# Block places of a group: one load of 14 from memory, five loads of three into ScalarE's registers, in place of two loads of seven each

## The chip, the cores and the metric

The kernel runs on one core of a Trainium2 chip. The metric is the time of one execution on the device in microseconds; the time before is the median of eight runs, 3712.68 us (3709.05 to 3725.59).

## The reference, cut to what matters

12,500 nodes with 32 features each, 400,000 edges sorted by their target `dst`. Two graph layers follow one another, each with a residual and a normalisation over the features:

```python
# layer 0: spline convolution, nine weight matrices blended per edge
messages = einsum('ek,ei,kio->eo', basis(edge_attr), x[src], weight)
out = zeros.at[dst].add(messages) / max(degree, 1)
x = layernorm(x + out + x @ root_w.T + root_b)
# layer 1: relational convolution, four bases weighted by the edge's type
for b in range(4):
    out = out + segment_sum((x[src] @ W[b]) * edge_type_weight[b][edge_type], dst)
x = layernorm(x + out)
```

The hard part is `x[src]`: every edge reads the row of its source node.

## The kernel before, in words

Most edges are cut into groups of 2304 (128 partitions by 18 columns, `GE`), 125 groups in all (`NG`). The setup sorts each group's edges by source; then the edges of a block of seven times 128 nodes lie next to each other. Layer 0 takes 92 of the groups (the first 33 are left to another path, the near work below), layer 1 all 125.

`layer(which)` loops over the groups. For each group `take(g)` makes 14 blocks (`NBL`), and for each block `block(k)` does this:

- At the first block of each half (`LOADS`, seven blocks each), SyncE's queue (SP) starts a load of the half's slot rows, `sl` (L1308, 1064 KB, two buffers), and a load of its seven block places, `hd` (L1312, 28 bytes, two buffers). Then ScalarE's queue loads the seven places from `hd` into its registers (L1314), with the order hint to stand behind the last move but one.
- At the first block of each quarter (`PIECES`, three or four blocks) VectorE compares the slot rows with the partition's number, which gives the 0/1 matrix `s` (L1324).
- TensorE multiplies seven node tiles by `s` into one of three PSUM banks (L1334): the rows of the block's sources, in sorted order.
- ScalarE moves the bank into `yt` (L1341), at a place that is known only when the kernel runs. A register holds it: two register operations split it into the place in `yt` and the place in the bank, and the move uses both. This is "the move" below, 14 a group.

`use(g)` takes the finished `yt` in three pieces of six columns, spread over the blocks of the next group: TensorE turns the piece back to edges (`y`, L1354), VectorE compares edges with targets (`hot`, L1366) and multiplies by the edges' coefficients (`outer`, L580), and TensorE sums by target (`agg`, L1389). After the third piece ScalarE copies the sum out (`agg_sb`, L599), TensorE applies the weights (L605), ScalarE and VectorE store the result in three parts (`rows`, L587 to L590), and later "hit" matmuls (L742) add it to the nodes' totals. The near work gathers the edges that belong to no group by indirect DMA (L124) and sums them by matmuls of L1079; it runs beside both layers.

The instructions of each engine are put in order by a planner when the kernel is built, from the order of the calls, the buffers and the hints (`issue_after`). Each engine then runs its list in order: an instruction that waits holds up all behind it. A load into registers occupies ScalarE's own queue. Where the load is behind a waiting copy, it starts when that copy has started.

The names that matter: `heads` (pool of `hd`), `begins` (the registers by block), `moves` (the list of moves), `banks` (three), `LOADS`, `PIECES`, `begin_d` (the places in memory, 125 rows of 14).

## Time and profile before

| | |
|---|---|
| median of 8 runs | 3712.68 us |
| the profiled execution | 3717.11 us |
| its span, first to last instruction | 3714.6 us |
| TensorE / VectorE / GpSimd / ScalarE busy | 77% / 81% / 70% / 57% |
| layer 0, 776 to 2270 us: TensorE / ScalarE busy | 1411 / 877 us of 1494 |
| layer 1, 2320 to 3680 us: TensorE / ScalarE busy | 1241 / 724 us of 1360 |
| loads of places into registers (L1314) | 434, median 967 ns |
| loads of places from memory (L1312) | 434 |
| moves (L1341) | 3038, median 383 ns |

The busy time of an engine counts what its datapath does. Loads into registers and register arithmetic run in the engine's queue (ACTq for ScalarE); they show in the chain and in the answers on a single line, not in the busy time. Where the profile says that an engine was idle until "issue", its queue was occupied with such things.

### The profile page before, as it was taken

How to read it: one execution, taken by the hardware profiler on the slowest of the kernel's cores; microseconds unless marked ns; L12 is line 12 of the kernel's file. 1: busy time of each engine (PE TensorE's matmuls, PEld its weight loads, DVE VectorE, ACT ScalarE, POOL GpSimd, SP SyncE). 2: the span in 40 equal slices, each digit the busy share in tenths (PEclk: the TensorE clock that was granted, in tenths of full speed). 3: DMA queues.
4: the chain of work that ended last, by engine and by line, in shares of the span. 5: the costliest groups of instructions: out<-in, count | busy, mean ns of one | idle time of the engine just before them, and what ended most of it. 6: DMA issues, size and time to landing. Idle time of an engine off the chain costs nothing.

```text
span 3714.6 us, 110703 instructions
## 1 busy us (share of the span) xinstructions
PE 2868.4 (77%) x40674; PEld 2458.3 (66%) x40674; DVE 3000.6 (81%) x5847; ACT 2103.4 (57%) x5610; POOL 2598.3 (70%) x2393
## 2 busy tenths in 40 slices
PE   2222221159999999999999997889999999989997
PEld 1121111147777777777777775888888888888886
DVE  5899979579899999986777775777777778878786
ACT  4688866345556665655566553555555555555553
POOL 4767777727777777777777771676777777777730
PEclk9955555579999999999999997999999999999998
DMA  4000001155556555555555453666776677777663
GB/s 93 14 11 14 14 14 14 31 176 160 166 166 180 167 167 172 176 164 152 155 168 154 146 165 108 212 214 207 218 224 214 213 229 219 220 218 219 204 224 100
DMA packets 202776, 564.88 MB, mean 152 GB/s; under 512 B 75796, under 2 KB 141944, under 8 KB 146170
## 3 DMA queue, kind: packets, MB, share of 16 engines
q1 hardware_dynamic: 123924, 511.77, 43.6%
q0 software_dynamic: 75888, 40.38, 6.3%
q8 instruction: 319, 5.23, 0.6%
q10 hardware_dynamic: 2410, 5.59, 0.6%
q14 instruction: 235, 1.93, 0.2%
HBM read 531.76 MB, written 25.76 MB: 150 GB/s over the span
## 4 chain that ended last, share of the span: by engine, by line
PE 53%; POOL 7%; ACT 5%; issue 5%; DVE 4%; ACTq 3%; DMA 3%; SPq 0%; POOLq 0%; DVEq 0%
PE agg L1389 26%; PE bank L1334 19%; POOL n_xg L124 7%; ACT yt L1341 3%; ACTq L1314 3%; PE y L1354 2%; PE n_bank L1079 1%; DMA n_xg<-in_x_dram,n_idx 1%; PE wg L876 1%; ACTq L1341 1%; ACT agg_sb L599 1%; PE wg L1105 1%; PE n_sum L742 1%; DMA z_dram<-n_z 1%; DVE hot L1376 1%
## 5 line engine op out<-in xcount | busy, mean ns | idle before, releaser
L124 POOL DMA_INDIRECT n_xg<-in_x_dram,n_idx x1469 | 1628.5, 1109 | 561.5 <-issue 433.1
L1341 ACT ACTIVATE yt<-bank x3038 | 1162.7, 383 | 553.7 <-PE bank L1334 320.9
L1389 PE MATMUL agg<-hot,outer 128*128 128x82 f32 (+1 forms) x7812 | 1413.4, 323 | 5.1 <-DVE hot L1376 3.8
L1334 PE MATMUL bank<-s,x 128*128 128x108 bf16 (+3 forms) x21266 | 1174.6, 202 | 189.4 <-ACT yt L1341 159.6
L1334 PEld LDWEIGHTS <-x 128*128 128x128 bf16 x21266 | 1007.4, 98 | 339.1 <-issue 226.1
L124 POOL DMA_INDIRECT n_xg<-z_dram,near_i x875 | 938.6, 1073 | 383.9 <-issue 256.9
L1389 PEld LDWEIGHTS agg<-hot,outer 128*128 128x128 f32 (+1 forms) x7812 | 1071.8, 181 | 128.9 <-DVE hot L1376 6.1
L1324 DVE TENSOR_SCALAR s<-sl,row 128x1824 bf16<-128x1824 int16 x868 | 679.1, 784 | 147.9 <-PE bank L1334 119.0
L1376 DVE TENSOR_TENSOR hot<-agg,hot_b 128x984 f32<-128x984 f32 x276 | 324.9, 1177 | 105.2 <-ACT agg_sb L599 56.4
L580 DVE TENSOR_TENSOR outer<-co,y 128x768 f32<-128x768 f32 x375 | 354.5, 945 | 0.0
L1079 PE MATMUL n_bank<-n_w,n_xg 128*32 128x72 f32 x3024 | 140.8, 256 | 199.0 <-DMA n_xg<-in_x_dram,n_idx 96.0
L1366 DVE TENSOR_TENSOR hot<-in_order,y 128x492 f32<-128x492 bf16 x375 | 248.0, 661 | 50.4 <-PE y L1354 46.6
L599 ACT ACTIVATE agg_sb<-agg 128x82 f32<-128x82 f32 (+1 forms) x217 | 64.5, 297 | 332.3 <-PE agg L1389 316.5
L1079 PEld LDWEIGHTS n_bank<-n_w,n_xg 128*32 128x32 f32 x3024 | 81.3, 121 | 244.6 <-DMA n_xg<-in_x_dram,n_idx 115.2
L1374 ACT ACTIVATE hot<-hot_b 128x492 f32<-128x492 bf16 x276 | 167.3, 606 | 116.7 <-PE agg L1389 91.3
L1354 PE MATMUL y<-add,yt 96*128 96x32 bf16 x3906 | 218.9, 177 | 4.1 <-DVE outer L580 4.1
L245 ACT ACTIVATE in_order<-src,thr 125x2304 bf16<-125x2304 int16 x97 | 213.9, 2205 | 0.7
L1354 PEld LDWEIGHTS <-yt 96*128 96x128 bf16 x3906 | 179.8, 98 | 13.5 <-issue 7.4
L580 DVE TENSOR_TENSOR outer<-co_b,y 128x384 f32<-128x384 f32 x276 | 151.0, 547 | 30.1 <-ACT outer L1373 28.2
L1062 DVE TENSOR_TENSOR n_w<-n_basis,n_hot 128x864 f32<-128x864 f32 x162 | 136.8, 850 | 18.7 <-PE n_bank L1079 18.4
L1259 DVE SCALAR_TENSOR_TENSOR co<-eq,etw_sb,co 128x180 f32<-128x180 f32 (+1 forms) x364 | 128.0, 390 | 2.0
L739 DVE TENSOR_SCALAR n_hit<-cols,place_of 82x128 bf16<-82x128 f32 (+2 forms) x301 | 100.3, 346 | 19.4 <-PE n_sum L742 19.1
(266 smaller groups left out, 2826.7 us busy)
## 6 DMA issues: line engine op xcount, KB each, us to landing
sl<-slots SPq DMA_DIRECT2D x434, 1064.0 KB
n_xg<-in_x_dram,n_idx POOLq DMA_INDIRECT x1469
n_xg<-z_dram,near_i POOLq DMA_INDIRECT x875
z_dram<-n_z SPq DMA_DIRECT2D x49, 256.0 KB
hd<-begin_d SPq DMA_DIRECT2D x434, 0.0 KB
co_d<-co SPq DMA_DIRECT2D x13, 360.0 KB
co<-co_d SPq DMA_DIRECT2D x13, 360.0 KB
args_t<-args_d SPq DMA_DIRECT2D x25, 90.0 KB
```

The lines of the kernel that those rows point to most:

```text
L124: return nc.gpsimd.indirect_dma_start(out=xg, out_offset=None, in_=table, in_offset=bass.IndirectOffsetOnAxis(ap=idx, axis=0))
L245: nc.scalar.activation(t, of[:NG], AF.Sign, bias=bias, scale=scale, accum_out=total)
L580: return nc.vector.tensor_tensor(t[:, :c, at:at + k * D].rearrange("p c (k d) -> p c k d", k=k), co[:, :, :, None].to_broadcast([P, c, k, D]),
L1079: nc.tensor.matmul(o, self.xg[i][:, at[0], at[1], :], v, start=True, stop=True, tile_position=(0, j * D))
L1324: nc.vector.tensor_scalar(s[:, :n], slots_of[k][:, :n], row, None, op0=ALU.is_equal)
L1334: nc.tensor.matmul(bank[:, AHEAD + a:AHEAD + b], parts[:, w * M3:w * M3 + P], s[:, off_[j]:off_[j + 1]], start=(j == 0), stop=(j == B - 1) ...
L1341: moves.append(nc.scalar.activation(yt[:M3, ds(to, LONG)], bank[:M3, ds(place, LONG)], AF.Copy))
L1354: nc.tensor.matmul(y[:, c, :], yt[:M3, k * P:(k + 1) * P], add3[:M3, :], start=True, stop=True)
L1366: nc.vector.tensor_tensor(hot.rearrange("p c (m i) -> p c m i", i=2), rel.to_broadcast([P, SUB, MAXR // 2, 2]), (col_ps if which else col_ ...
L1374: nc.scalar.activation(spread[:, :, 0, :], hot, AF.Copy)
L1376: nc.vector.tensor_tensor(spread[:, :, 1:, :], b0[:, :, :, None].to_broadcast([P, SUB, 2, MAXR]), hot[:, :, None, :].to_broadcast([P, SUB, ...
L1389: near.behind = nc.tensor.matmul(agg[0], t[:, c, :], v, start=(k == 0), stop=(k == CH - 1)).ins
```

## The change

The places get a load of their own: at the first block of a group, `hd` takes all 14 from memory in one DMA. Into ScalarE's registers they go three at a time, at blocks 0, 3, 6, 9 and 12 (the last time two). The slot rows stay in two loads a group. The order hint of the register load is the same as before. Nothing that is computed changes.

```diff
-            co_of = {}
+            co_of, hd_of = {}, {}
...
                 def block(k):
+                    if k == 0:
+                        hd_of[g] = heads.tile([1, NBL], I32, name="hd")
+                        nc.sync.dma_start(hd_of[g], begin_d[g:g + 1, :])
+                    if k % 3 == 0:
+                        n = min(3, NBL - k)
+                        with tc.issue_after(moves[-2].ins) if len(moves) > 1 else ExitStack():
+                            _, v = nc.values_load_multi_w_load_instructions(
+                                hd_of[g][:, k:k + n], engines=[mybir.EngineType.Activation],
+                                min_val=0, max_val=GE * BANK + AHEAD,
+                                skip_runtime_bounds_check_because="counted, and bounded")
+                        begins.update(zip(range(k, k + n), v))
                     for k0, k1 in LOADS[which]:
                         if k == k0:
...
-                            hd = heads.tile([1, NBL // 2], I32, name="hd")
-                            nc.sync.dma_start(hd[:, :k1 - k0], begin_d[g:g + 1, k0:k1])
-                            with tc.issue_after(moves[-2].ins) if len(moves) > 1 else ExitStack():
-                                _, v = nc.values_load_multi_w_load_instructions(
-                                    hd[:, :k1 - k0], engines=[mybir.EngineType.Activation],
-                                    min_val=0, max_val=GE * BANK + AHEAD,
-                                    skip_runtime_bounds_check_because="counted, and bounded")
-                            begins.update(zip(range(k0, k1), v))
                             slots_of.update({i: sl[:, (i - k0) * WS:] for i in range(k0, k1)})
```

In the built order ScalarE's list has 1085 register loads of places where it had 434, and SP's list 217 loads of `hd` where it had 434. The planner also places other work anew: in layer 1 the copy of `agg` stands ahead of the eighth move in 106 of 125 groups before, and ahead of the second move in 98 of 125 groups after.

## Prediction

> **What bounds the kernel now.** I read the page's busy table first, then the chain that ended last, then the two layers apart. TensorE carries the largest share of the chain, 53%. The setup before about 776 us holds no step of this change, so only the two layers count: 92 groups of 14 blocks from about 776 to 2270 us (layer 0) and 125 from about 2320 to 3680 us (layer 1).

> ```profile
> PE 2868.4 (77%) x40674; PEld 2458.3 (66%) x40674; DVE 3000.6 (81%) x5847; ACT 2103.4 (57%) x5610; POOL 2598.3 (70%) x2393
> ...
> PE 53%; POOL 7%; ACT 5%; issue 5%; DVE 4%; ACTq 3%; DMA 3%; SPq 0%; POOLq 0%; DVEq 0%
> ```

> The chain of waits, taken for 2330 to 3640 us alone, has this sum by line. The register load of the block places (ACTq L1314) is 6.0% of 1310 us there, 79 us, and the moves behind it another 4.9%. The longest waits of TensorE in the same stretch, and in 790 to 2260 us, name one cause each time: a block can't start because ScalarE hasn't emptied its bank.

> ```profile
> by line: PE bank L1334 38.2%; PE agg L1389 38.0%; ACTq L1314 6.0%; ACT yt L1341 4.9%; PE y L1354 3.6%; issue 2.9%; ACT agg_sb L599 2.0%; PE n_bank L1079 1.4%; ACTq L1341 1.4%; PE n_sum L742 0.4%; DVE hot L1366 0.2%; DVE outer L580 0.2%; DVE
> ```

> ```profile
> PE bank L1334 <- ACT yt L1341: 111.9, 126, 1.4
> ```

> ```profile
> PE bank L1334 <- ACT yt L1341: 44.4, 98, 1.9
> ```

> So layer 1 has one such wait a group (126 in 120 groups or so), 0.89 us each; layer 0 has half as much a group. The timeline of one group of layer 1 shows how it comes about.

> ```profile
> 3002.81 0.24 ACT L599 ACTIVATE agg_sb<-agg 128x82 f32<-128x82 f32 x1 [1.72 <-PE agg L1389]
> ...
> 3004.10 0.80 ACT L1341 ACTIVATE yt<-bank  x2 [1.05 <-issue]
> ...
> 3004.54 0.44 PE L1334 MATMUL bank<-s,x 128*128 128x108 bf16 x7 [1.10 <-ACT yt L1341]
> ```

> ScalarE stands at the copy of agg until TensorE is done, then its queue loads seven places (968 ns, unseen by the busy time), and only then the eighth move of the group runs. TensorE has three banks, so its eleventh block waits for that move, 1.10 us here. In the built order of before, 106 of 125 groups of layer 1 have exactly this sequence: copy of agg, load, eighth move. The group's other load lies behind the last move of the group before, while TensorE does agg products, and no wait follows it.

> **What one load costs.** Two pairs of moves of ScalarE with a load between them:

> ```profile
> L1314 ACTq TENSOR_LOAD <-hd x1: 962/962/962, 3006.6 to 3006.6; - x1
> ```

> ```profile
> 3006.19 0.80 ACT L1341 ACTIVATE yt<-bank  x2
> 3007.88 0.80 ACT L1341 ACTIVATE yt<-bank  x2 [0.90 <-PE bank L1334]
> ```

> The gap is 0.90 us; between moves without a load it is 0.03 (five moves take 2.04 us, 0.414 apart, 0.383 each). (The view names a block as releaser; the block had come, and the load ended at 3007.57.) So a load of 7 values costs ScalarE 0.87 us, 0.09 less than its 0.96, since the queue starts it while the move ahead still runs.

> The trace has no load of three. It is bounded by the loads it has: all 434 of hd take about 967 ns for seven values, and the one-value loads at the end of the kernel are these.

> ```profile
> L1314 ACTq TENSOR_LOAD <-hd x434: 956/967/1969, 776.0 to 3674.8; - x145
> ```

> ```profile
> L1626 SPq TENSOR_LOAD <-again x1: 553/553/553, 2331.3 to 2331.3; - x1
> ...
> L1626 ACTq TENSOR_LOAD <-again x1: 288/288/288, 3704.8 to 3704.8; - x1
> L1626 DVEq TENSOR_LOAD <-again x1: 543/543/543, 3705.4 to 3705.4; - x1
> ```

> Lower end 288 ns (count doesn't matter, the short row is the price), upper end 967 ns (count doesn't matter, the long row is). In between: a straight line through ScalarE's own two rows gives (967-288)/6 = 113 ns a value, so 514 ns for three and 401 for two; a line from the other queues' 553 gives 69 ns a value and 691 for three. I take 514, since both its rows are ScalarE's; it costs 0.42 us in the row of moves, the load of two 0.31.

> [...]

> **The change part by part.**
> 1. Loads on ScalarE a group: before 2 x 0.87 = 1.74 us, after 4 x 0.42 + 0.31 = 1.99 us, so +0.25. Bounds: 5 x 0.20 = 1.0 (-0.74) and 5 x 0.87 = 4.35 (+2.61). The register arithmetic of the moves is unchanged (three instructions for each of 3038 moves); 651 loads are added (434 become 1085).
> 2. Layer 1, what goes: in the built order of after, the copy of agg comes ahead of the second move in 98 of 125 groups, and no load stands directly behind it. The wait of the eleventh block goes, -0.89 us a group. From the eighth block on TensorE now does three blocks, then y and agg (12 agg matmuls at about 0.11 us each, 1.34, and y 0.16): 3 x 0.28 + 1.50 = 2.3 us, against three moves and a load on ScalarE, 3 x 0.414 + 0.42 = 1.66. ScalarE catches up there.
> 3. Layer 1, what comes: blocks 1 to 8 have no such pause between them. The seventh block needs the fourth move, and ScalarE has ahead of that, from the copy of agg on: the copy 0.27, two moves 0.83, rows 0.21, a load 0.42, the fourth move 0.38 and 0.05 to TensorE, 2.16 us. TensorE meanwhile has four blocks 1.12, y 0.16, the weights 0.14, and on average 0.15 of hit matmuls: 1.57, of which 0.25 passed before the copy began. That leaves 0.6 to 0.85 us, and up to 1.15 where rows waits for the weights' matmul; the near work (1736 matmuls of L1079 in 125 groups, in runs of 28) takes some away where it falls in between. I take 0.69, so -0.20 us a group, times 125: -25 us. The bounds are 0.4 (-61 us) and 1.15 (+32).
> 4. Layer 0: TensorE is busy 1397 of 1470 us, and ScalarE has more idle time. The 44.4 us of waits stand against 184 loads x 0.87 = 160 us, so 28% of load time reaches TensorE. +0.25 x 92 x 0.28 = +6 us.
> 5. The DMAs of places: 434 of 7 become 217 of 14, each some 0.24 us of SP's issue. In the trace SP sits behind the register loads (575.6 us in 217 waits in layer 1) and nobody waits for that but the slot rows. Now the places wait for the last of five loads, ahead of the second slot load of the group in SP's built order; that load's data are used more than half a group later. VectorE waited for slot rows only 14.6 us in 23 waits in layer 1, so the cover is thin there but it holds: 0. Bounds: -15 us, and 0.7 us a group later, +88, if every part of it showed.

> Sum: -25 + 6 = -19 us. The profiled execution took 3717.1 us (span 3714.6), 4.4 above the median of the runs shown; its sum would be 3698, and against the median of 3712.7 it is 3694.

> **Rivals.**
> - Forecast, 3694, chance 0.53. Its own range is 3665 to 3712, most of the bounds in part 3 with loads near 0.5 us.
> - The price of three values lies midway between the two lines, at 0.60 us: each load costs 0.51, a group 2.49 (+0.75). The seventh block's wait grows by 0.09, so layer 1 gives -14, layer 0 +0.75 x 92 x 0.28 = +19: 3718, no change that shows within its own spread. Chance 0.12.
> - Slower: a load costs ScalarE nearly the same whatever it carries, and the load ahead of the fourth move becomes the wait that the eleventh block had. It decides from about 0.57 us for three values. At 0.69: a group pays 4 x 0.60 + 0.53 = 2.93 (+1.19), layer 0 +31, layer 1 -25 + 0.18 x 125 = -3, together 3741. At 0.967 ScalarE itself bounds layer 1: 14 moves 5.8, loads 4.35, copy and rows 0.7, near work 0.3, 11.2 us and some waiting that it can't fill, against 10.9 now (1360 us over 125); I put +0.85 us a group, 106, and layer 0 +2.61 x 92 x 0.28 = 67: 3886. For it speak the other queues' 490 to 553 ns for one value; against it ScalarE's 288. Chance 0.31, a third of it near the top.
> - The wait of SP: slot rows late in layer 1, +0.3 us a group, 3731. Chance 0.04.
> - That the change doesn't do what it says is excluded by the built order: 1085 loads, 217 DMAs.

> **How the numbers follow.** A measurement of this kernel can tell about 0.2%, 7.4 us, from no change. Below 3705 lies the forecast but for the upper end of its own range, and a little of the second case where the bounds of part 3 and of part 5 help it: faster, 0.53. Same, the rest of these two: 0.13. Slower, the third and fourth, less what of them stays near 3712: 0.34. The range goes from 3660 to 3770; it leaves out the top of the slower case (0.10) and as much beyond the gain of the forecast and in the tails.

> **What would show it.** Right: ScalarE's register loads near 514 ns for three; the wait of TensorE's blocks for moves in layer 1 below 112 us, now at the seventh block and not the eleventh; layer 0 within 10 us. Wrong: loads of 600 ns and more; more waits of blocks for moves in layer 0; VectorE waiting for slot rows for over 30 us.

## The result and the profile after

The changed kernel takes 3758.39 us, the median of 14 runs (3741.21 to 3783.26); beside it the kernel before takes 3714.45 (40 runs). The ratio is 1.0121, interval [1.0108, 1.0134]: slower, where the forecast was faster. Eight of the runs below (e5 to e8 and e13 to e16) were made on two other chips, where the kernel before itself took 6206 and 6162 us and TensorE, VectorE and ScalarE stand still together again and again in every profile, for 5 to 43 us (near 4110 us of e6 TensorE stood 15.1 us, ScalarE 19.4, VectorE 23.6; the cause is not known); of these runs the ratios to that kernel are given, and otherwise only their groups at full clock are read.

The profiled execution took 3767.13 us (span 3764.6), 50.0 more in span than before. From the start of a layer's first move to that of its last, layer 0 went from 1478.1 to 1502.6 us (+24.5), layer 1 from 1404.5 to 1439.5 (+35.0); the setup and what lies between and behind the layers took 9.5 less. The busy table and the chain of the page:

```profile
PE 2870.0 (76%) x40674; PEld 2484.7 (66%) x40674; DVE 3008.8 (80%) x5847; ACT 2153.0 (57%) x5610; POOL 2564.4 (68%) x2393
...
PE 58%; ACT 9%; ACTq 5%; issue 4%; DVE 3%; DMA 2%; SPq 0%; POOL 0%; DVEq 0%
```

The work is the same; ScalarE and its queue have a larger part of the chain. The chain for 2330 to 3640 us by line, then TensorE's longest waits in 2340 to 3640 us and in 790 to 2260 us (sum, times, longest):

```profile
by line: PE agg L1391 36.5%; PE bank L1336 31.9%; ACT yt L1343 7.9%; ACTq L1308 4.7%; issue 4.0%; PE y L1356 3.7%; ACTq L1343 1.7%; ACT agg_sb L599 1.6%; PE n_bank L1079 1.5%; ACT rows L587 1.3%; DMA sl<-slots 1.3%; PE wg L605 1.2%; PE n_su
```

```profile
PE bank L1336 <- ACT yt L1343: 127.2, 168, 1.5
```

```profile
PE bank L1336 <- ACT yt L1343: 95.9, 200, 2.7
```

Blocks still wait for moves and for hardly anything else. In layer 0 these waits doubled (44.4 us before), in layer 1 they grew a little (110.9 before, in the same stretch). And this is what one register load costs (minimum, median, maximum, ns):

```profile
L1308 ACTq TENSOR_LOAD <-hd x1085: 493/703/1990, 769.5 to 3730.4; - x181
```

That is the median of all loads: three values take 706 ns, two 497. The prediction had 514 and 401. All loads of places together occupy ScalarE's queue for 733 us, before 432.

**Layer 0.** The timeline of ScalarE at a change of groups, the load there, and TensorE's fourth block:

```profile
848.14 0.61 ACT L1376 ACTIVATE hot<-hot_b 128x492 f32<-128x492 bf16 x1 [1.95 <-PE agg L1391]
849.16 0.38 ACT L1343 ACTIVATE yt<-bank  x1 [0.41 <-PE bank L1336]
```

```profile
L1308 ACTq TENSOR_LOAD <-hd x1: 709/709/709, 848.1 to 848.1; - x1
```

```profile
849.60 0.44 PE L1336 MATMUL bank<-s,x 128*128 128x108 bf16 x7 [0.66 <-ACT yt L1343]
```

The copy waits 1.95 us for TensorE's sums, the load behind it in the queue starts with the copy and ends at 848.85, and only then comes the group's first move, for which the fourth block waits 0.66 us. In the built order of before, the load stands ahead of that copy here: at the same change of groups it started at 848.4, 3.0 us ahead of the group's first block, and the fourth block waited 0.14:

```profile
L1314 ACTq TENSOR_LOAD <-hd x1: 967/967/967, 848.4 to 848.4; - x1
```

```profile
851.58 0.62 ACT L1374 ACTIVATE hot<-hot_b 128x492 f32<-128x492 bf16 x1 [1.11 <-PE agg L1389]
...
852.10 0.36 ACT L1341 ACTIVATE yt<-bank  x1
```

```profile
851.38 1.58 PE L1334 MATMUL bank<-s,x 128*128 128x108 bf16 x28
```

There the first move follows the copy at once, and the four blocks run as one row. Fourth blocks waited some 21 us in layer 0 before and 60 after; tenth blocks 2.4 and 23.

**Layer 1.** One group, ScalarE's timeline, the load in it, and the seventh block of TensorE:

```profile
3022.48 0.24 ACT L599 ACTIVATE agg_sb<-agg 128x82 f32<-128x82 f32 x1
3022.74 0.80 ACT L1343 ACTIVATE yt<-bank  x2
3023.95 0.19 ACT L587 ACTIVATE rows<-wg 82x32 bf16<-82x32 f32 x1 [0.41 <-PE wg L605]
3024.98 1.22 ACT L1343 ACTIVATE yt<-bank  x3 [0.83 <-ACT rows L587]
```

```profile
L1308 ACTq TENSOR_LOAD <-hd x1: 707/707/707, 3024.0 to 3024.0; - x1
```

```profile
3025.42 0.85 PE L1336 MATMUL bank<-s,x 128*128 128x108 bf16 x14 [1.09 <-ACT yt L1343]
```

The wait is where the prediction put it, at the seventh block, and for its reason: the copy of agg, two moves, rows waiting for the weights' product, and behind it the load (0.83 us without a move). It came to some 118 us in all, where the eleventh block's had been 109.

That alone is no loss: the groups of layer 1 at full clock take 10.82 us (105 of them), before 10.83 (114). The 35 us are in the others. From the fifth group on, those touched by a lowered TensorE clock are 15 with 13.56 us, before 6 with 12.37: 15 x 2.74 = 41 us more than at full clock, before 6 x 1.54 = 9. The half-clock time in layer 1, counted from 40 us behind its first move, is 123 us, before 35. (In the kernels before and after the clock is lowered in the layer's first group too, from 2288 to 2329 and from 2305 to 2343 us.) The view by stretches (busy us and instructions of the five engines, then the granted clock):

```profile
2359.70:2366.50 6.80, 6.80 (x67) 6.80 (x63) 4.47 (x7) 2.20 (x7) 5.28 (x6) 0.50 0.45 146
2366.50:2373.30 6.80, 5.40 (x93) 5.07 (x92) 3.66 (x7) 3.58 (x12) 5.28 (x6) 1.00 0.68 199
2373.30:2380.20 6.90, 6.90 (x70) 6.90 (x66) 4.39 (x7) 2.29 (x8) 5.38 (x6) 0.51 0.52 150
2380.20:2387.00 6.80, 5.39 (x93) 5.06 (x91) 3.73 (x7) 3.62 (x12) 5.28 (x6) 1.00 0.69 196
```

The clock drops to 0.50 for 6.8 us and is back at 1.00 for 6.8, again and again. At half clock TensorE is busy all the time, at full clock it idles 1.4 us of 6.8. Behind the layer's first group all the lowered stretches in the trace of the kernel after are 3.41, 6.83, 10.24 or 23.89 us long, that is 1, 2, 3 or 7 times 3.41.

### The profile page after: what moved, and what is told of

The parts are those of the page before. It is cut to its first block, busy times and chain, and to the rows that moved or that the text cites. A ratio compares the mean times of both kernels' runs of the same rounds, so it can differ in the third digit from the quotient of the medians.

```text
span 3764.6 us, 110775 instructions
## 1 busy us (share of the span) xinstructions
PE 2870.0 (76%) x40674; PEld 2484.7 (66%) x40674; DVE 3008.8 (80%) x5847; ACT 2153.0 (57%) x5610; POOL 2564.4 (68%) x2393
## 4 chain that ended last, share of the span: by engine, by line
PE 58%; ACT 9%; ACTq 5%; issue 4%; DVE 3%; DMA 2%; SPq 0%; POOL 0%; DVEq 0%
PE agg L1391 31%; PE bank L1336 18%; ACT yt L1343 6%; ACTq L1308 3%; PE y L1356 2%; PE n_bank L1079 2%; ACTq L1343 2%; ACT hot L1376 1%; PE wg L876 1%; PE wg L605 1%; PE wg L1105 1%; PE n_sum L742 1%; DMA sl<-slots 1%; ACT agg_sb L599 1%; ACT rows L587 0%
## 5 line engine op out<-in xcount | busy, mean ns | idle before, releaser
L1391 PE MATMUL agg<-hot,outer 128*128 128x82 f32 (+1 forms) x7812 | 1447.3, 327 | 5.4 <-DVE hot L1378 3.7
L1336 PE MATMUL bank<-s,x 128*128 128x108 bf16 (+3 forms) x21266 | 1188.5, 203 | 265.0 <-ACT yt L1343 237.1
L1336 PEld LDWEIGHTS <-x 128*128 128x128 bf16 x21266 | 1026.1, 100 | 397.9 <-issue 321.9
L124 POOL DMA_INDIRECT n_xg<-z_dram,near_i x875 | 919.0, 1050 | 457.5 <-issue 255.7
L1391 PEld LDWEIGHTS agg<-hot,outer 128*128 128x128 f32 (+1 forms) x7812 | 1110.3, 185 | 132.9 <-issue 7.0
L580 DVE TENSOR_TENSOR outer<-co,y 128x768 f32<-128x768 f32 x375 | 354.5, 945 | 0.0
L1079 PE MATMUL n_bank<-n_w,n_xg 128*32 128x72 f32 x3024 | 131.0, 255 | 181.5 <-DMA n_xg<-in_x_dram,n_idx 78.1
L1079 PEld LDWEIGHTS n_bank<-n_w,n_xg 128*32 128x32 f32 x3024 | 77.8, 121 | 221.4 <-DMA n_xg<-in_x_dram,n_idx 92.6
L1356 PEld LDWEIGHTS <-yt 96*128 96x128 bf16 x3906 | 174.8, 98 | 10.9 <-issue 5.2
L580 DVE TENSOR_TENSOR outer<-co_b,y 128x384 f32<-128x384 f32 x276 | 151.1, 547 | 36.4 <-ACT outer L1375 35.1
L1062 DVE TENSOR_TENSOR n_w<-n_basis,n_hot 128x864 f32<-128x864 f32 x162 | 136.4, 848 | 18.5 <-PE n_bank L1079 13.8
L599 ACT ACTIVATE agg_sb<-agg 128x82 f32<-128x82 f32 (+1 forms) x217 | 64.6, 297 | 123.4 <-PE agg L1391 117.0
L742 PEld LDWEIGHTS <-n_hit 82*128 82x128 bf16 (+1 forms) x905 | 72.7, 108 | 64.8 <-DVE n_hit L739 51.9
```

The source lines that it names most:

```text
L124: return nc.gpsimd.indirect_dma_start(out=xg, out_offset=None, in_=table, in_offset=bass.IndirectOffsetOnAxis(ap=idx, axis=0))
L580: return nc.vector.tensor_tensor(t[:, :c, at:at + k * D].rearrange("p c (k d) -> p c k d", k=k), co[:, :, :, None].to_broadcast([P, c, k, D]),
L1079: nc.tensor.matmul(o, self.xg[i][:, at[0], at[1], :], v, start=True, stop=True, tile_position=(0, j * D))
L1336: nc.tensor.matmul(bank[:, AHEAD + a:AHEAD + b], parts[:, w * M3:w * M3 + P], s[:, off_[j]:off_[j + 1]], start=(j == 0), stop=(j == B - 1) ...
L1356: nc.tensor.matmul(y[:, c, :], yt[:M3, k * P:(k + 1) * P], add3[:M3, :], start=True, stop=True)
L1391: near.behind = nc.tensor.matmul(agg[0], t[:, c, :], v, start=(k == 0), stop=(k == CH - 1)).ins
```

## The experiments

"Half clock" below is the time in layer 1 at the lowered clock, counted as above, and every layer time is of a run's profiled execution.

**e1_sizes: what a load costs by its size and start.** The places are loaded by a plan that changes with the group:

```diff
-                    if k % 3 == 0:
-                        n = min(3, NBL - k)
+                    plan = ((14,), (7, 7), (3, 3, 3, 3, 2), (4, 4, 4, 2), (5, 5, 4), (6, 8), (1, 13), (9, 5))[g % 8]
+                    at = [sum(plan[:i]) for i in range(len(plan))]
+                    if k in at:
+                        n = plan[at.index(k)]
```

> One DMA of 14 places a group, as in the changed kernel, but the register loads carry other numbers of values in turn, by group: 14 / 7,7 / 3,3,3,3,2 / 4,4,4,2 / 5,5,4 / 6,8 / 1,13 / 9,5. It measures the price of one load by its number of values. Known: 285 ns for one, 497 for two, 703 for three, 967 for seven. Theory A (a price that rises by some 209 ns a value while few are asked for, and more slowly beyond): four between 0.75 and 0.92 us, five to eight near 0.97 to 1.1, fourteen between 1.2 and 1.9. Rival B (a straight line through one and seven, the prediction's): 4 at 0.63, 5 at 0.74, 14 at 1.76. Rival C (a line of 209 ns a value from one on, and seven an oddity): 4 at 0.91, 5 at 1.12, 6 at 1.33, 8 at 1.75, 14 at 3.0.

One execution, 3773.17 us. Medians of the register loads, by number of values and first value, us:

| values, start | us | values, start | us |
|---|---|---|---|
| 1 at 0 | 0.288 | 7 at 0 | 0.971 |
| 2 at 12 | 0.500 | 7 at 7 | 1.550 |
| 3 at 0, 3, 6, 9 | 0.702 to 0.710 | 8 at 6 | 1.750 |
| 4 at 0, 4, 8 | 0.310 to 0.328 | 9 at 0 | 0.788 |
| 4 at 10 | 0.920 | 13 at 1 | 2.824 |
| 5 at 0 / 5 / 9 | 0.552 / 1.132 / 1.117 | 14 at 0 | 1.241 |
| 6 at 0 | 0.771 | | |

**e2_merge7 and e3_two_dmas: the two parts of the change apart.** e2 is the change with one DMA of 14 places, but two register loads of seven (n = 7 at blocks 0 and 7). e3 has the loads of three, but two DMAs of seven places.

```diff
-                    if k % 3 == 0:
-                        n = min(3, NBL - k)
+                    if k % 7 == 0:
+                        n = 7
```

> The DMA part of the change alone: one DMA of 14 places a group, and still two register loads of seven. The built order is nearly that of the kernel before. If the register loads carry the whole loss: within 0.2% of the kernel before, 3714 us, with the wait of TensorE's blocks for moves at about 111 us in layer 1 and 44 in layer 0. If the later load of places or the slot rows behind it in SP's queue carry part of it: over 3722.

> The register part alone: the places come in two DMAs of seven a group, both started at the group's first block, and go to the registers three at a time. The built order is nearly that of the changed kernel. If the register loads carry the whole loss: 3758 us, 1.012 of before, within its own spread of 3741 to 3783. If the merged DMA carries part: below 3740.

e3: ratio 1.0210 [1.0159, 1.0261], layer 0 1500.5, layer 1 1447.7 us, half clock 132, waits as in the kernel after (58.2 us at fourth blocks of layer 0, 122.2 at seventh blocks of layer 1). So the register loads make the loss without the merged DMA. (That e3 is 0.9% slower still than the kernel after, 3766 to 3808 us in four executions, stays unexplained.) e2: 4023.81 us, ratio 1.0846 [1.0820, 1.0872], the slowest of all. It was no clean test of the DMA, for its second load starts at value 7 and takes 1.55 us; layer 1 took 1692.7 us, 598 of them at half clock.

**e6, e10 (merge7_at8): the DMA alone. e7 (seven_at1): the price alone.** In merge7_at8 a group has 16 places of storage, one DMA, and two loads of seven at values 0 and 8. In seven_at1 the kernel before has its second seven stored from value 1 of their tile; its order of instructions is that of before.

```diff
-                            hd = heads.tile([1, NBL // 2], I32, name="hd")
+                            o = 1 if k0 else 0
+                            hd = heads.tile([1, 8], I32, name="hd")[:, o:]
```

> The kernel before with only the DMA part of the change: one DMA of 16 places, two register loads of seven at offsets 0 and 8, both multiples of four, each expected at 0.965 us as before. Theory P (the DMA part is worth nothing; in the run with the merged DMA and the second load at offset 7 the loss came from that load's 1.55 us): 3700 to 3725, register-load total within 10 us of 432, waits at the eleventh block in layer 1 as before (105 to 115 us). Rival R (the merged DMA itself, its landing or its place on SP's queue, costs time): over 3750, and the waits would name the DMA queue.

> The DMA part alone, again on another chip: one DMA of 16 places a group, two register loads of seven at offsets 0 and 8. Theory P: the DMA part is worth nothing, 3700 to 3725, register-load total within 10 us of 432, wait at the eleventh block in layer 1 of 105 to 115 us. Rival R (the merged DMA costs time by itself): over 3750, the waits naming the DMA.

> The kernel before with both DMAs and its order unchanged, but the second seven places of a group stored from value 1 of their tile, so that their register load reads seven values from a start that is no multiple of four: by the run with mixed sizes 1.55 us instead of 0.965. Theory P (price of the load alone, 0.58 us a group in the stall at the eleventh block, and then the granted clock): 3980 to 4040, layer 1's half-clock time 500 to 650 us, wait at the eleventh block 1.3 to 1.5 us a group. Rival R (the merged DMA was the cause in the earlier run): 3700 to 3730. A third case, that the stall lengthens but the clock doesn't follow: 115 groups of layer 1 times 0.58 = 67 us, 3775 to 3790.

e10: 3726.17 us, ratio 1.0034 [1.0023, 1.0044]; e6 1.0006 [0.9987, 1.0024]. Layer 1 is as before (1406.7 us, eleventh block 108.1, half clock 46), but not so layer 0: 1493.5 us, with 59.2 us at fourth blocks. With the places' DMA called at the group's first block, ahead of the slot rows, the planner puts the group's first load behind the waiting copy (in e3, with two DMAs called there, it does too), and that costs a third of a per cent. Rival R falls, and theory P is missed by a little: the DMA part is not quite worth nothing.

e7, on one of those two chips: 1.0380 [1.0353, 1.0406]; 111 of 120 groups of layer 1 are touched by the lowered clock (61 in e6, on that chip). The time by which e7 was expected at 3980 to 4040 can't be read there; that the price alone costs, with one order and no merged DMA, can. The cleanest pair is e2 and e10, with the same order of instructions on TensorE and ScalarE. Here are the loads of both in layer 0 and 1 together, then the stretch 2340 to 3580 us, first e2, then e10:

```profile
L1308 ACTq TENSOR_LOAD <-hd x434: 956/1532/2271, 775.1 to 3982.3; - x145
```

```profile
L1310 ACTq TENSOR_LOAD <-hd x434: 957/966/1722, 772.7 to 3690.1; - x145
```

```profile
2340.00:3580.00 1240.00, 1092.73 (x15785) 1051.00 (x15785) 791.69 (x1422) 538.18 (x1639) 740.80 (x707) 0.82 0.58 177
```

```profile
2340.00:3580.00 1240.00, 1130.46 (x19450) 1068.79 (x19449) 968.04 (x1756) 659.42 (x2008) 928.68 (x866) 0.99 0.71 217
```

Every second load takes 0.58 us longer (e2's 1532 is the middle of two kinds, 0.97 and 1.55). Over 125 groups of layer 1 that is 73 us; layer 1 grew by 286, and the clock fell from 0.99 to 0.82. The longer wait accounts for 73 us once, and the clock came with some three times as much.

**e8, e11 (filler): is it the pause that lowers the clock?** e2 with eight more products in the place where TensorE waits; nothing uses their result.

```diff
+            if layer:
+                at[0] = wide()[:MAXR, :D]
+                for _ in range(8):
+                    filled[layer] = nc.tensor.matmul(at[0], s[:k, :MAXR], w1_sb, start=True, stop=True)
...
+                        with tc.issue_after(filled[1].ins) if k == 10 and 1 in filled else ExitStack():
```

> The kernel with the merged DMA and two loads of seven at offsets 0 and 7 (4024 us, layer 1 1693 us, 598 us of it at half clock), with eight extra matrix products in each of layer 1's groups that read the aggregate and whose result nothing uses, placed in the order just ahead of the eleventh block, where TensorE waits for the second load. Theory S (the idle stretch of about 1.4 us in each group is what brings the lowered clock, and the lowered clock is what costs the time): half-clock time in layer 1 under 300 us and time under 3880. Rival T (the clock is lowered for another reason, or the products merely add to the time): half-clock time over 450 us and time of 4000 or more.

> Again on another chip: the kernel with the merged DMA and two loads of seven at offsets 0 and 7 (4024 us, 598 us of layer 1 at half clock), with eight extra matrix products a group of layer 1, whose result nothing uses, where TensorE waits ahead of the eleventh block. Theory S (the idle stretch of some 1.4 us a group brings the lowered clock): half-clock time in layer 1 under 300 us, time under 3880. Rival T (the clock is lowered for another reason, or the products only add): half-clock time over 450 us, time 4000 or more.

e11: 3868.48 us, ratio 1.0411 [1.0377, 1.0445], half clock 121 us: more work for TensorE, and 155 us less than e2. Theory S holds: with the pause filled, most of the half clock goes (598 us in e2), and with e2 against e10 (598 and 46) that makes the pause what lowers the clock in these runs. (The planner also moved the weights' product from behind the tenth block to behind the fourteenth, so the order is not e2's throughout. e8: 1.0250 [1.0222, 1.0279].) A rule of how much pause is too much did not come out: TensorE's idle time in layer 1's groups and the half clock stood at 112 and 35 us in the kernel before, 139 and 123 after, 142 and 33 in e9 below, 77 and 121 in e11. The length of the single pause fits better: from the fifth group of layer 1 on, the traces have 5 pauses of TensorE over 1.2 us before, 39 after, 1 in e9, none in e17 and 92 in e2. But the 1.2 us are picked afterwards, and e11 has 4, so this is a hint and no rule.

**e5, e9 (padded): five cheap loads.** The places are stored three to a stretch of four, and each load takes four values from a multiple of four.

```diff
-                                hd_of[g][:, k:k + n], engines=[mybir.EngineType.Activation],
+                                hd_of[g][:, k // 3 * 4:k // 3 * 4 + 4], engines=[mybir.EngineType.Activation],
```

> The kernel after, with the 14 places of a group stored three to a stretch of four values (20 places of storage, one DMA), so that each register load reads four values from a start that is a multiple of four: five loads in the same places of the order, each expected at 0.325 us by the run with mixed sizes, instead of 0.703 for three and 0.497 for two. Theory P (the time of one register load sets the loss, first by layer 0's moves, then by a longer stall in layer 1 that lowers the granted clock): register loads fall from 733 to about 340 us; layer 0's waits of the block products for moves are at most 44 us, layer 1's under 70; the half-clock time of layer 1 falls from 123 to under 40 us; time 3640 to 3690. Rival Q (the number of loads or their places between the moves sets the loss, whatever one costs): 3740 to 3780, waits as in the kernel after.

> The kernel after with the 14 places of a group stored three to a stretch of four values, so that each of the five register loads reads four values from a start that is a multiple of four; a repeat on another chip, because on the first one the kernel before itself took 6206 us and all four engines but GpSimd stood without instructions for stretches of some 20 us. There the loads took 0.314 us each. Theory P (the time of one register load sets the loss): layer 0's waits of the block products for moves at most 44 us, layer 1's under 70, half-clock time of layer 1 under 40 us, time 3640 to 3690. Rival Q (the number of loads or their places set it): 3740 to 3780, waits as in the kernel after.

> The kernel with five loads of four values (3756 us, loads of 0.314 us), its order of instructions unchanged on TensorE and ScalarE, but with the places stored from value 1, so that no load starts at a multiple of four: by the run with mixed sizes each then takes 0.92 us. Theory P (in layer 0 the group's first load stands on TensorE's path, so the wait of the fourth block is the load's time less some 0.05 us): that wait rises from about 0.26 to about 0.87 us a group, from 13 to some 70 us in layer 0, and layer 0 from 1473 to 1520 to 1550 us. In layer 1, if the load counts there too, 113 full-clock groups of 11.27 us grow by 0.3 to 0.6 us, and the half-clock time grows with the waits: 3850 to 4050 in all. Rival Q (the place of a load in the order decides, its time hardly): under 3790, waits within 20 us of those of the padded kernel.

e9: 3756.22 us, ratio 1.0113 [1.0084, 1.0142] (e5: 1.0063 [1.0047, 1.0080]). This was a miss: the time is the one that rival Q had. Layer 0 did what theory P says: 1473.1 us, fourth blocks 13.0. Layer 1 did not: 1457.8 us with only 33 us of half clock, its groups at full clock 11.27 us. With loads of four in place of three the planner made another order: in layer 1 the weights' product stands behind the group's first block in 74 of 125 groups, where it mostly stood behind the fifth, and waits came at the second, fourth and seventh block and at y, 1.17 us a group. So e9 shows the price in layer 0, and in layer 1 an order that waits as much as that of the kernel after.

e13 keeps e9's order and shifts the places by one value, so that every load is priced singly. The loads of e9 and of e13:

```profile
L1311 ACTq TENSOR_LOAD <-hd x1085: 303/308/1307, 770.8 to 3720.4; - x181
```

```profile
L1311 ACTq TENSOR_LOAD <-hd x1085: 900/911/1897, 897.9 to 6552.2; - x181
```

0.60 us more. In layer 0's groups at full clock the fourth block's wait goes from 0.26 to 0.86 us (medians of e5 and e13, both on the chips set apart above), 0.60 more: all that the load got dearer reaches TensorE. With the 0.66 of the kernel after (0.709 in the group above) and the 0.92 of most waits in e10 (0.966), the wait is the load's time less 0.05. Layer 1's groups at full clock go from 11.25 (e5) to 13.20, the ratio to 1.0688 [1.0658, 1.0717]. Rival Q fell. But only 14 groups of layer 1 are left at full clock, and they grew by 1.95 us where 0.3 to 0.6 was expected.

**e14, e18 (l0_ahead), e15 (l1_ahead), e16, e17 (both): the place alone.** Loads of three at 0.703 us throughout. In l0_ahead the group's first load is called at the last block of the group before, its DMA at that group's block 7, and layer 0's copies are hinted behind it:

```diff
+                    if k == 7 and g + 1 < NG:
+                        heads_of(g + 1)
...
+                    if k == 13 and g + 1 < NG:
+                        places(g + 1, 0)
...
+                        with tc.issue_after(newest[0].ins):
+                            nc.scalar.activation(t[:, :, :D], y, AF.Copy)
+                            nc.scalar.activation(spread[:, :, 0, :], hot, AF.Copy)
```

In l1_ahead, with the same earlier DMA, layer 1's loads are called one block earlier, and its first rows copy is hinted behind the newest load.

```diff
+                    if which and k % 3 == 2 and k + 1 < NBL:
+                        places(g, k + 1)
...
+        with tc.issue_after(newest[0].ins) if behind else ExitStack():
+            nc.scalar.activation(r[:, 0], v, AF.Copy)
```

> The kernel after with the same five loads of three (0.703 us each), but the load of a group's first three places is called at the last block of the group before, its transfer from memory half a group earlier, and in layer 0 ScalarE's copies of the products (which wait for TensorE) are hinted to stand behind it, so that the load no longer stands behind a waiting copy. Theory P: the price is paid in ScalarE's idle time, layer 0's wait at the fourth block falls from 60 to under 25 us, layer 0 from 1502.6 to 1470 to 1485 us; layer 1 is as in the kernel after (wait at the seventh block, 100 to 130 us of half clock): 3725 to 3750 in all. Rival: five loads of three cost ScalarE too much wherever they stand, layer 0 stays over 1495 and the time at 3750 or more.

> The edit in layer 0 alone, again on another chip. Theory P: wait of the fourth block under 25 us in layer 0 (60 in the kernel after), layer 0 1470 to 1485 us, layer 1 with a wait of 100 to 130 us at the seventh block and 60 to 200 us of half clock: 3725 to 3755. Rival: layer 0 over 1495 us.

> The kernel after with the same five loads of three; in layer 1 each load is called one block earlier, and ScalarE's copies of the weighted sums, which wait for TensorE's weights product, are hinted to stand behind the newest load. Layer 0's calls are as in the kernel after, but for the transfer from memory half a group earlier. Theory P (in layer 1 the stall at the seventh block is the chain of weights product, waiting copy, load behind it, move): the wait at the seventh block falls from 118 to under 40 us, no other block's takes its place, the half-clock time falls from 123 to under 30 us, layer 1 from 1439 to 1310 to 1360 us, the time to 3630 to 3690. Rival (the loads' total of 3.3 us a group is what ScalarE cannot hold): the wait moves to another block, layer 1 over 1400 us, time over 3720.

> Both of the foregoing edits together. If they are independent, the sum of their gains: layer 0 1470 to 1485 us, layer 1 1310 to 1360 us, time 3600 to 3665; against the kernel with one load of 14 (3623 us) it tells whether the number of loads costs anything once none of them stands behind a waiting copy. Rival (the number of loads costs by itself): over 3665.

> Both edits of the place together (loads of three at 0.703 us, in layer 0 ahead of the copies that wait for TensorE, in layer 1 ahead of the copies of the weighted sums), on another chip than before, where the kernel before itself took 6162 us; there layer 1's undisturbed groups took 10.29 us against 10.83 of the kernel before and 10.82 of the kernel after. Theory P: layer 1 at 10.3 us a group is 1310 to 1340 us with under 30 us of half clock, layer 0 1470 to 1485 us, time 3600 to 3650. Rival (a loss that the undisturbed groups don't show): over 3690.

e18: 3705.82 us, ratio 0.9979 [0.9962, 0.9997]. The fourth blocks' wait fell from 60.0 to 4.1 us as theory P says; but tenth blocks went from 23.0 to 52.3, and layer 0 stopped at 1490.9 us, between P and its rival. Its groups at full clock take 16.01 us (after 16.47, before 15.96). Layer 1 changed too, which was not expected: its first load now stands ahead of the last move, the seventh block waits 105.9 us, half clock 53, layer 1 1397.6. e14: 1.0018 [1.0000, 1.0035].

e17: 3661.98 us, ratio 0.9872 [0.9840, 0.9904], 1.3% below the kernel before with the same five loads of three that lost 1.2%. TensorE's longest waits in 790 to 2260 and in 2340 to 3640 us:

```profile
PE bank L1352 <- ACT yt L1359: 68.3, 122, 1.8
```

```profile
PE bank L1352 <- ACT yt L1359: 67.3, 129, 1.1
```

Layer 1 takes 1353.0 us and no group from its fifth on meets a lowered clock. Both numbers miss the expectation by a little (1340, and 3650 for the whole): the seventh block still waits 59.3 us. e15 (0.9995 [0.9976, 1.0014]) and e16 (0.9964 [0.9946, 0.9981]) have layer 1's groups at full clock at 10.27 and 10.29 us, 10.51 in e17; e6, on one of the two chips set apart, has 10.84. Against e4 below, with one load a group, e17 is some 39 us slower, and layer 1 differs by as much (1353.0 and 1314.0): five loads, or the waits that their places still bring, cost that.

**e4_one14, e12_one16: one load a group.** n = 14 at block 0; and n = 16 with storage of 16.

```diff
-                    if k % 3 == 0:
-                        n = min(3, NBL - k)
+                    if k == 0:
+                        n = NBL
```

> One DMA and one register load of 14 values a group, at the group's first block, behind the last move of the group before, where TensorE does agg products. No load lies behind the copy of agg any more. Theory (the number of loads and their place set the time): if the load takes under 1.9 us, the wait of the eleventh block in layer 1 goes, and the kernel is faster than before, 3630 to 3700. Rival (what ScalarE pays in sum sets the time): 1.9 us against 2 x 0.97 is no gain, 3705 to 3720; at 3 us it is slower, over 3760.

> One DMA of 16 values and one register load of 16, start and length multiples of four, at the head of the group, where the kernel with one load of 14 (3623 us) has its load of 1.241 us. By the law of the run with mixed sizes (0.325 for the first four, about 0.245 for each further four, about 0.21 for each single value left over) it takes 0.33 + 3 x 0.245 = 1.06 us against 1.24. Theory P: 0.18 us x 217 groups on ScalarE, partly covered behind the aggregate's products: 3600 to 3623. Rival: covered wholly, 3620 to 3626. If the values go one by one whatever the start, 3.4 us and a time over 3700.

e4: 3622.94 us, ratio 0.9767 [0.9749, 0.9785], a little below what was expected. e12: 3629.64, ratio 0.9766 [0.9745, 0.9786]: its load takes 1.02 us for e4's 1.23 and brings nothing more, as the rival has it; the rest of that price is covered. Waits and stretch of e4 in layer 1, 2340 to 3640 and 2340 to 3580 us:

```profile
PE bank L1336 <- ACT yt L1343: 11.5, 53, 0.7
```

```profile
2340.00:3580.00 1240.00, 1213.29 (x20829) 1129.02 (x20827) 1032.40 (x1890) 706.16 (x2144) 917.45 (x864) 1.00 0.72 230
```

The one load stands behind the last move of the group before, while TensorE is at agg products; none is left in the middle of a group. Layer 1 takes 1314.0 us, and in the stretch shown the clock is 1.00 and TensorE is busy 1213 us of 1240. This is the best version found, 2.3% below the kernel before.

| | ratio | load, us | layer 0 | layer 1 | half clock |
|---|---|---|---|---|---|
| before | 1 | 0.967 | 1478.1 | 1404.5 | 35 |
| after | 1.0121 | 0.703 | 1502.6 | 1439.5 | 123 |
| e2, 7 and 7 from one DMA | 1.0846 | 0.97, 1.55 | 1497.8 | 1692.7 | 598 |
| e10, the same, aligned | 1.0034 | 0.966 | 1493.5 | 1406.7 | 46 |
| e9, five of four | 1.0113 | 0.308 | 1473.1 | 1457.8 | 33 |
| e17, five of three, ahead | 0.9872 | 0.703 | 1477.9 | 1353.0 | 19 |
| e4, one of 14 | 0.9767 | 1.227 | 1474.1 | 1314.0 | 7 |

## Why the prediction was wrong

- **The price of a load of three (part 1): the step that failed.** "I take 514": 703 measured. (The 703 is the median of all five; threes alone are 706.) The line through ScalarE's rows of one and seven values mixed two prices: by e1 the seven were priced as a four and three singles, and three are all singles. With 703 and 497 in the prediction's own sum a group pays 4 x 0.61 + 0.41 = 2.85 us (+1.11), layer 0 gives +29 and layer 1 -1: 3740, slower, where the forecast was 3694. The bounds 288 and 967 held the price. The line from the other queues' 553 ns, set aside as not ScalarE's, gave 691 by luck. Both first signs of being wrong came: loads over 600 ns, and more waits in layer 0.
- **The slower rival had the direction and two thirds of the size.** At 0.69 it gave 3741: layer 0 +31, layer 1 -3. Measured: layer 0 +24.5, layer 1's groups at full clock -0.01 us each, some -1. That its layer 0 came near is luck, as the point on layer 0 says.
- **The clock (no step of the prediction).** Layer 1's other +36 us came with half-clock time, 35 to 123 us. The page of before showed 0.99 in layer 1, and I took the waits at their own length only. e2 against e10 shows that a longer wait in an unchanged order does this (598 us of half clock against 46), and e11 that with the pause filled most of it goes (121). For the kernel after itself this is argued from them and from e17 (wait 0.47 us a group, half clock 19 us), not shown by a run in its own order. How much pause the clock bears stays open, and with it why the kernel after got 123 us and e9 only 33; that after has 39 pauses over 1.2 us and e9 one is a hint.
- **Layer 1's waits (parts 2 and 3): right in kind.** The eleventh block's wait went and the seventh's came, by the chain that was named. 118.4 us over 125 groups is 0.95 us; 0.69 + 0.19 for the dearer load is 0.88. e17 shows the chain from the other side: with the load ahead of the rows copy it is 0.47. The sign that was set, waits below 112 us, failed all the same (127).
- **Layer 0 (part 4): wrong by more than the price.** A share of 28% of load time was carried over from before, though the built order had the group's first load behind a copy that waits for TensorE; e13 shows that such a load reaches TensorE whole, less 0.05 us. The named waits grew by 51.5 us and the layer by 24.5; half-clock time in layer 0 fell by 22 us, which may be part of the difference; it isn't resolved.
- **SP (part 5): right.** VectorE's waits for slot rows in layer 1 went from 13.8 us to 9.5.

## What to carry to other kernels

Price a load into registers by its start and its size together: here one load of 14 from a multiple of four values (1.23 us) was cheaper than five of three and two (3.3 us a group), and three values (0.70) cost more than four (0.31) and nearly three quarters of seven (0.97). Look where it stands in its engine's list: behind an instruction that waits for TensorE, all but 0.05 us of its time was on the path (0.86 us of 0.91 in e13), and an edit of the transfers can move it there through the planner (e10: 59.2 us at fourth blocks). Where TensorE waits once in each short group, price what its clock does as well as the wait (e2: loads longer by 73 us, layer 1 by 286), above all when groups at full clock show no loss.

## What the hardware showed that I had not expected

- A load of four values from a multiple of four took 0.31 us (e9), about what a load of one took (0.29, e1); one of three 0.70 (the kernel after), one of 14 1.23 (e4), one of 16 1.02 (e12).
- A load 0.58 us longer in each group of 10.8 us brought TensorE to half clock for 598 us of 1693 (e2 against e10). In the kernel after the lowered stretches of layer 1 were whole multiples of 3.41 us; where two low and two full ones alternated, the groups took about 13.7 us, close to four times 3.41.
